# A 5x5 convolution written as 64x64 tensor tiles, with one PSUM bank's halves exchanged

## Chip, cores and metric

The kernel runs on one core of one Trainium2 chip. The metric is the device time of one launch in microseconds (us). All data are float32.

## What is computed

Four layers, each of the form x = x + f(normalised x), on a tensor of 8 batches, 32 channels, 256 rows, 256 columns. The change lies in layer 1, fused with the end of layer 0:

```python
x = x + _L0_conv_ref(_gn(x), ...)            # Fourier layer, 32x32 kept modes
x = x + _L1_conv_ref(_gn(x), kernel, 1, 2)   # layer 1: the same 5x5 kernel for every channel
x = x + _L2_conv_ref(_gn(x), ...)            # recurrence along the columns
x = x + _L3_conv_ref(_gn(x), ...)            # running maxima in four directions, mixed

def _gn(v, G=16, eps=1e-5):                  # groups of two channels
    m, s = mean(g), var(g)                   # over the group's channels and the image
    return (g - m) / sqrt(s + eps)

out = lax.conv_general_dilated(Xf, kernel[None, None], window_strides=(1, 1), padding=[(2, 2), (2, 2)])
```

## The kernel before

The program has four stages: `forward_and_mix` (forward transform and spectral product), `inverse_and_conv` (inverse transform of layer 0 and the whole of layer 1), `recurrence` (layer 2) and `maxima_and_mix` (layer 3). Only `inverse_and_conv` changes. All four keep the order written in the program: within an engine nothing overtakes anything, and the framework adds the semaphore waits.

**Data.** An image is cut into nine blocks of 32 columns that overlap by four, so that 28 of each are new. A partition is (row modulo 4, column in the block): four groups of 32 partitions. The 64 other rows, `q`, lie along the free dimension, with a zero at either end. Eight channels of nine blocks form one buffer `x1`; five such buffers rotate. A unit `u` is 16 channels of a batch, that is two buffers (`ch` 0 and 1); there are 16 units. A group of two channels is one step `g`, 0 to 7, and a step works on 9 blocks x 2 channels x 64 rows = 1152 columns.

**Convolution.** Because a partition holds row modulo 4 and column, the 5x5 kernel is a 128x128 matrix on one column of data, plus a correction for the taps that reach into the row group before or behind. In step `g`, `conv_within` (line 469) multiplies with the whole 128x128 matrix into three PSUM banks of 256, 512 and 384 columns (`BANKS`), and `conv_across` (line 477) adds the correction by two 64x64 matrices per bank, from the lower 64 partitions into the upper and the other way, with the data shifted by one row. Then VectorE (line 488) computes x = PSUM * r + x in place, with r the reciprocal standard deviation and a running sum of the result, and ScalarE (`squares2`, line 494) sums the squares. The PSUM tiles `vp` have four buffers, handed out in turn, three to a step.

**The inverse transform of the next unit** goes on beside it. `over_rows` (line 408, on `tp`, one buffer, copied out by ScalarE) works on the unit two ahead. `transform(u + 1, p, ...)` calls `over_columns` for block `p` (line 425, eight 64x32 matmuls into the two buffers of `up`), and VectorE adds the old x (line 433). `BEFORE` and `BEHIND` place the nine transforms of a unit: those of `BEFORE[g]` stand between `conv_within` and `conv_across`, those of `BEHIND[g]` after `conv_across`. `scale` (lines 456 to 462) computes r; `statistics` (lines 519 to 536) the moments for layer 2, with a power on GpSimd in it; `spectrum` (lines 366 to 380) prepares a batch's spectrum, in every second unit. SyncE's queue stores the finished buffers (line 507), GpSimd's queue loads the old x (line 387).

Of the kernel before, what the change touches and what calls it, by code (L numbers as in the profile page):

```python
# [9 lines left out]
F32 = mybir.dt.float32  # L10
AF = mybir.ActivationFunctionType
ALU = mybir.AluOpType
# [4 lines left out]
P = 128  # L17
# [7 lines left out]
Q = H // A  # L25
# [275 lines left out]
def inverse_and_conv(tc, k, d, smd, xmean, x2d, stb, first):  # L301
# [12 lines left out]
    BANKS = ((0, 2), (2, 6), (6, 9))  # L314
    PIECES = ((0, 3), (3, 6), (6, 9))

    BEFORE = ((0,), (2,), (4,), (6,), (7,), (8,), (), ())
    BEHIND = ((1,), (3,), (5,), (), (), (), (), ())
    with ExitStack() as ctx:
        one = ctx.enter_context(tc.tile_pool(name="a2c", bufs=1))  # L320
        xp = ctx.enter_context(tc.tile_pool(name="a2x", bufs=1))
# [18 lines left out]
        def x1_of(u, ch):  # L340
            return x1s[(2 * u + ch) % 5][0]

        def pair_of(u, ch, g, lo, hi, q0=1, rows=slice(0, P)):

            return x1s[(2 * u + ch) % 5][1][rows, 2 * lo : 2 * hi, g, q0 : q0 + Q]
# [71 lines left out]
        def over_columns(u, p, tag="up", bufs=2):  # L417


            tt = state[u]["tt"]  # L420
            ups = [ps.tile([P, CH * Q], F32, name=f"up_{u}_{p}_{ch}", tag=tag, bufs=bufs) for ch in range(2)]
            for a in range(A):
                for ch in range(2):
                    r = slice(64 * ch, 64 * ch + 64)
                    nc.tensor.matmul(  # L425
                        ups[ch][32 * a : 32 * a + 32],
                        lhsT=k.gw[r, p, :],
                        rhs=tt[r, a].rearrange("p c q -> p (c q)"),
                        start=True,
                        stop=True,  # L430
                    )
            for ch in range(2):
                nc.vector.tensor_tensor(  # L433
                    x1_of(u, ch)[:, p, :, 1 : 1 + Q],
                    ups[ch].rearrange("p (c q) -> p c q", q=Q),
                    xs.pop((u, ch, p)),
                    ALU.add,
                )

        def squares(u, ch, n, lo, hi, vector=False):  # L440
# [21 lines left out]
            nc.gpsimd.tensor_tensor(r, ve, k.mhalf[:, :G], ALU.pow)  # L462
            state[u]["r"][ch] = r

        def conv_within(u, ch, g):
            vps = []
            for lo, hi in BANKS:
                vp = ps.tile([P, 2 * (hi - lo), Q], F32, name=f"vp_{u}_{ch}_{g}_{lo}", tag="vp", bufs=4)
                nc.tensor.matmul(vp, lhsT=k.conv[:, 0:P], rhs=pair_of(u, ch, g, lo, hi), start=True, stop=False)  # L469
                vps.append(vp)  # L470
            return vps

        def conv_across(u, ch, g, vps):
            for (lo, hi), vp in zip(BANKS, vps):

                for r, o, q0 in ((slice(0, 64), slice(64, 128), 2), (slice(64, 128), slice(0, 64), 0)):
                    nc.tensor.matmul(  # L477
                        vp[o],
                        lhsT=k.conv[r, P : P + 64],
                        rhs=pair_of(u, ch, g, lo, hi, q0, r),  # L480
                        start=False,
                        stop=True,
                    )
            s1 = state[u]["s1"]
            srcs = ((0, 1, vps[0][:, 0:2]), (1, 2, vps[0][:, 2:4]), (2, 6, vps[1]), (6, 9, vps[2]))
            for n, (lo, hi, src) in enumerate(srcs):
                x = pair_of(u, ch, g, lo, hi)
                nc.vector.scalar_tensor_tensor(  # L488
                    x, src, state[u]["r"][ch][:, g : g + 1], x, ALU.mult, ALU.add, accum_out=s1[:, 0, n, ch, g : g + 1]
                )  # L490

        def squares2(u, ch, g):
# [19 lines left out]
        def statistics(u):  # L512
# [17 lines left out]
            nc.vector.tensor_tensor(ve, st[:, 1], ve, ALU.subtract)  # L530
            nc.vector.tensor_scalar(ve, ve, 0.0, EPS, ALU.max, ALU.add)
            nc.gpsimd.tensor_tensor(st[:, 1], ve, k.mhalf[:, :n8], ALU.pow)
            for kind in range(2):
                nc.vector.tensor_copy(
                    by_pair(stb[:, kind, b, 2 * CH * h : 2 * CH * (h + 1)]), twice(st[:, kind], 2)
                )
# [15 lines left out]
        with tc.manual_schedule(engines=None):  # L552
# [18 lines left out]
                scale(0, ch, 3)  # L571
            for u in range(n):
                for g in range(2 * G):
                    vps = conv_within(u, g // G, g % G)
                    if u + 1 < n:
                        for p in BEFORE[g]:
                            transform(u + 1, p, u + 2)
                    conv_across(u, g // G, g % G, vps)
                    if u + 1 < n:
                        for p in BEHIND[g]:  # L580
                            transform(u + 1, p, u + 2)
                    squares2(u, g // G, g % G)
                    if g == 1 and u > 0:
                        scale(u, 1)
                    if g == 2:
                        if u > 0:
                            statistics(u - 1)
                        if u % 2 == 0 and u + 2 < n:
                            spectrum(units[u + 2][0])
                    if g == G and u + 2 < n:  # L590
                        begin(u + 2)
                    if g >= G and u + 2 < n:
                        over_rows(u + 2, 2 * (g - G))
                    if g == 5 and u + 1 < n:
                        squares(u + 1, 0, 1, 1, NT)
                    if g == 7 and u % 2 and u + 3 < n:
# [5 lines left out]
                if u + 1 < n:  # L602
                    scale(u + 1, 0)
                    squares(u + 1, 1, 1, 1, NT)
            statistics(n - 1)
            store(n - 1, 1)


def recurrence_weights(tc, pool, d):
# [525 lines left out]
```

## Time and profile before

| | |
|---|---|
| Time of three runs, median (lowest to highest) | 3248.49 us (3248.48 to 3251.19) |
| Profiled execution, its own time | 3246.24 us |
| Profiled execution, span | 3244.4 us |
| Mean granted TensorE clock | 0.937 |
| Stage of the change: first conv matmul to the last evacuation | 359.4 to 1149.6 us |
| TensorE busy in 359.4 to 1112.9 us | 750.0 of 753.5 us |
| VectorE busy there | 417.0 us |
| ScalarE busy there | 427.5 us |
| DMA engines' share there | 0.72 |

Engine names in the lines: PE is TensorE's matmuls, PEld its weight loads, DVE VectorE, ACT ScalarE, POOL GpSimd, SP SyncE. A busy PE means that some matmul was under way by a modelled end, not that the array was full. A float32 matmul appears as two records. "64*64" in a line is the part of the array used; "x12" the number of records merged into the line. The profiled span is 4.1 us below the median of the runs.

### The profile page before, as it was taken

To read this page: it belongs to the slowest core of one execution; us is meant where nothing else is said; L and a number is where in the kernel's file an instruction comes from. 1 tells how busy PE (TensorE), PEld (TensorE's weight loads), DVE (VectorE), ACT (ScalarE), POOL (GpSimd) and SP (SyncE) were. 2 spreads that over 40 slices of the span, in tenths; PEclk is the share of its full clock that TensorE was granted. 3 is DMA by queue.
4 is the path that set the end of the run, shared out by engine and by line. 5 is a ranking of instruction groups with operands and counts; after the bars stand their busy time and mean duration, and the time that the engine had idled before them with its cause. 6 is when DMAs were issued, how large, how long until landed. Compare 5 with 4: busy or idle time off the path is not lost.

```text
span 3244.4 us, 107343 instructions
## 1 busy us (share of the span) xinstructions
PE 2925.4 (90%) x45498; PEld 1658.2 (51%) x45498; DVE 2503.5 (77%) x4932; ACT 1851.6 (57%) x4362; POOL 861.9 (27%) x1241
## 2 busy tenths in 40 slices
PE   7975899999999969999999999999999577777776
PEld 4664344444443446666666666666666233333332
DVE  5742555555555548999999999899989799999998
ACT  3422456465564657888888888888888222222222
POOL 0110111111111135555555555555555200000000
PEclk9985899999999989999999999999999798888888
DMA  9978577687777546655555566665554577888885
GB/s 388 384 291 188 152 187 177 186 195 193 189 174 187 118 121 159 153 143 148 147 146 146 148 154 158 158 158 152 141 147 122 181 308 310 313 312 311 308 307 219
DMA packets 527038, 655.44 MB, mean 202 GB/s; under 512 B 388825, under 2 KB 389737, under 8 KB 500829
## 3 DMA queue, kind: packets, MB, share of 16 engines
q1 hardware_dynamic: 483628, 494.33, 53.9%
q0 software_dynamic: 17200, 85.05, 7.9%
q10 hardware_dynamic: 25728, 69.21, 5.4%
q8 instruction: 356, 5.83, 0.7%
q14 instruction: 126, 1.02, 0.1%
HBM read 371.63 MB, written 272.63 MB: 199 GB/s over the span
## 4 chain that ended last, share of the span: by engine, by line
PE 69%; DVE 20%; issue 4%; DMA 3%; SPq 1%; ACT 1%; POOL 0%; DVEq 0%; ACTq 0%; POOLq 0%
PE r L696 13%; PE z L696 12%; PE vp L469 8%; PE vp L477 8%; PE ni L696 6%; PE nh L696 6%; DVE rv L947 5%; PE up L425 4%; PE yp L131 3%; DVE dq L959 2%; DVE m L963 2%; DVE m L961 2%; DVE x L956 2%; DVE m L962 2%; PE tp L408 2%
## 5 line engine op out<-in xcount | busy, mean ns | idle before, releaser
L704 PE MATMUL z<-hs,weights 64*64 64x256 f32 x4080 | 540.8, 382 | 0.0
L704 PE MATMUL r<-hs,weights 64*64 64x256 f32 x4080 | 529.4, 375 | 1.6 <-issue 1.4
L704 PE MATMUL ni<-hs,weights 64*64 64x256 f32 x4080 | 528.0, 375 | 0.0
L786 POOL TENSOR_TENSOR xw<-xw,hs 128x256 f32<-128x256 f32 x496 | 339.4, 684 | 638.4 <-DVE hs L785 636.7
L993 ACT ACTIVATE ot<-o,bres 128x512 f32<-128x512 f32 x256 | 154.9, 688 | 541.6 <-PE o L977 536.4
L494 ACT ACTIVATE junk<-x 128x128 f32<-128x128 f32 (+1 forms) x384 | 202.7, 528 | 329.8 <-DVE x L488 323.4
L977 PE MATMUL o<-m,wsc 32*32 32x512 f32 x3072 | 242.8, 855 | 154.8 <-DVE m L963 109.0
L780 POOL TENSOR_TENSOR a<-zm,xn 128x256 f32<-128x256 f32 x510 | 372.3, 730 | 7.9 <-issue 6.2
L778 ACT ACTIVATE n<-n,bih 128x256 f32<-128x256 f32 x510 | 259.2, 508 | 188.9 <-DVE n L777 188.9
L433 DVE TENSOR_TENSOR x<-up,xb 128x512 f32<-128x512 f32 x288 | 185.2, 686 | 211.9 <-PE up L425 208.3
L696 PE MATMUL z<-xn,weights 64*64 64x256 f32 x2040 | 305.4, 376 | 23.8 <-ACT xn L676 23.8
L696 PE MATMUL r<-hs,weights 64*64 64x256 f32 x2040 | 319.0, 389 | 5.4 <-DVE hs L785 4.5
L488 DVE SCALAR_TENSOR_TENSOR x<-vp,r,x 128x128 f32<-128x128 f32 (+2 forms) x512 | 236.9, 514 | 110.3 <-PE vp L477 110.1
L696 PE MATMUL r<-xn,weights 64*64 64x256 f32 x2040 | 305.3, 376 | 1.4 <-ACT rs L771 1.4
L696 PE MATMUL z<-hs,weights 64*64 64x256 f32 x2040 | 305.9, 376 | 0.0
L696 PE MATMUL nh<-xn,weights 64*64 64x256 f32 x2040 | 305.7, 376 | 0.0
L696 PE MATMUL ni<-hs,weights 64*64 64x256 f32 x2040 | 305.0, 375 | 0.0
L469 PE MATMUL vp<-x,c_conv 128*128 128x256 f32 (+2 forms) x768 | 290.3, 512 | 1.9 <-DVE x L488 1.8
L704 PEld LDWEIGHTS ni<-hs,weights 64*64 64x64 f32 x4080 | 289.5, 133 | 3.0
L676 ACT ACTIVATE xn<-xw,shift,turned 128x256 f32<-128x256 f32 x496 | 290.6, 586 | 0.0
L704 PEld LDWEIGHTS r<-hs,weights 64*64 64x64 f32 x4080 | 282.5, 131 | 6.6 <-issue 4.9
L772 DVE SCALAR_TENSOR_TENSOR n<-nh,bhh,rs 128x256 f32<-128x256 f32 x510 | 246.4, 483 | 48.6 <-ACT rs L771 34.7
(167 smaller groups left out, 6585.9 us busy)
## 6 DMA issues: line engine op xcount, KB each, us to landing
xb<-in_xl_dram POOLq DMA_DIRECT2D x96, 768.0 KB, 5.9
xa<-in_xt_dram SPq DMA_DIRECT2D x64, 1024.0 KB
x<-x3d SPq DMA_DIRECT2D x32, 2048.0 KB
fw<-fwd SPq DMA_DIRECT2D x32, 2048.0 KB
out_dram<-ot ACTq DMA_DIRECT2D x64, 1024.0 KB
xw<-x2d SPq DMA_DIRECT2D x31, 2048.0 KB
fwd<-fm SPq DMA_DIRECT2D x248, 256.0 KB
x3d<-xw SPq DMA_DIRECT2D x248, 256.0 KB
```

The source lines that it names most:

```text
L469: nc.tensor.matmul(vp, lhsT=k.conv[:, 0:P], rhs=pair_of(u, ch, g, lo, hi), start=True, stop=False)
L477: nc.tensor.matmul(vp[o], lhsT=k.conv[r, P : P + 64], rhs=pair_of(u, ch, g, lo, hi, q0, r), start=False, stop=True,)
L488: nc.vector.scalar_tensor_tensor(x, src, state[u]["r"][ch][:, g : g + 1], x, ALU.mult, ALU.add, accum_out=s1[:, 0, n, ch, g : g + 1])
L494: nc.scalar.activation(junk[:, : 2 * (hi - lo)], pair_of(u, ch, g, lo, hi), AF.Square, accum_out=state[u]["s1"][:, 1, n, ch, g : g + 1],)
L676: nc.scalar.activation(norms[bi][:, b, w], raws[bi][:, b, w], AF.Identity, bias=shift[:, b : b + 1], scale=sc[:, 1, b : b + 1])
L696: ins = nc.tensor.matmul(out[r], lhsT=weights[r, kind, gate, :], rhs=src[r], start=start, stop=stop)
L704: ins = nc.tensor.matmul(out[pairs[1 - i]], lhsT=weights[r, kind, gate, :], rhs=prev[r, :, q0 : q0 + Q], start=False, stop=stop,)
L772: nc.vector.scalar_tensor_tensor(m, p["nh"], bhh[:, 2:3], r, ALU.add, ALU.mult)
L778: nc.scalar.activation(m, m, AF.Tanh, bias=bih[:, 2:3])
L780: product = nc.gpsimd.tensor_tensor(a, zm, cur, ALU.mult)
L786: nc.gpsimd.tensor_tensor(raw, raw, new, ALU.add)
L977: nc.tensor.matmul(pts[b2][i][32 * j : 32 * j + 32].rearrange("p (w q) -> p w q", q=Q), lhsT=wsc[q, b2, t, :], rhs=src[j][q, b2], start=first,
```

## The change

The 128x128 matrix is no longer used whole. For each of the three banks there are three kinds of 64x64 pair: kind 0, the two diagonal quarters of the matrix; kind 1, its two off-diagonal quarters; kind 2, the old corrections. Each pair takes two of the four 64x64 tiles of the array: either the two diagonal ones (rows of the lower half to outputs in the lower half, upper to upper) or the two crosswise ones. In the middle bank (512 columns) the two halves of the output are exchanged, so that its kinds 1 and 2 use the diagonal tiles and its kind 0 the crosswise ones. In program order diagonal and crosswise pairs of different banks alternate. A semaphore orders the pairs that add into one bank from different rows.

The evacuation has five VectorE instructions instead of four, in the order bank 2, middle bank (two of 64 partitions, each reading PSUM from the other half than the one it writes), bank 0 (two). The transforms come after a step's convolution, and where a step has two of them (steps 1, 2 and 3), `scale`, `statistics` or `over_rows` stands between. `over_rows` for the unit two ahead starts at step 3 instead of 4. `statistics` is split: its last two copies (`keep`) come after `squares2`.

```diff
-    BEFORE = ((0,), (2,), (4,), (6,), (7,), (8,), (), ())
-    BEHIND = ((1,), (3,), (5,), (), (), (), (), ())
+    PLACES = ((0,), (1, 2), (3, 4), (5, 6), (7,), (8,), (), ())
...
-        def conv_within(u, ch, g):
...
-        def conv_across(u, ch, g, vps):
...
+        pairs = (slice(0, 64), slice(64, 128))
+        sem, count = tc.alloc_semaphore("conv_tiles"), [0]
+        some = [False]
+        def free(ins):
+            if some[0]:
+                tc.declare_no_dep(ins.ins, group="conv", reason="later matmuls of the same bank end last")
+        def conv(u, ch, g):
+            vps = [
+                ps.tile([P, 2 * (hi - lo), Q], F32, name=f"vp_{u}_{ch}_{g}_{lo}", tag="vp", bufs=4) for lo, hi in BANKS
+            ]
+            def tiles(bank, kind, start=False, stop=False, signal=False, wait=None):
+                lo, hi = BANKS[bank]
+                for i, r in enumerate(pairs):
+                    o = pairs[i if kind == 0 else 1 - i]
+                    to = pairs[i if (kind == 0) != (bank == 1) else 1 - i]
+                    ins = nc.tensor.matmul(
+                        vps[bank][to],
+                        lhsT=k.conv[r, P : P + 64] if kind == 2 else k.conv[r, o],
+                        rhs=pair_of(u, ch, g, lo, hi, (2, 0)[i] if kind == 2 else 1, r),
+                        start=start,
+                        stop=stop,
                     )
+                    if wait is not None and i == 0:
+                        ins._wait_ge(sem, wait)
+                if signal:
+                    ins.then_inc(sem, 1)
+                    count[0] += 1
...
+            tiles(1, 1, start=True)
+            tiles(2, 1, start=True)
+            second = tiles(2, 2, signal=True)
+            first = tiles(1, 2, signal=True)
+            tiles(0, 1, start=True)
+            tiles(2, 0, stop=True, wait=second)
+            third = tiles(0, 2, signal=True)
+            tiles(1, 0, stop=True, wait=first)
+            tiles(0, 0, stop=True, wait=third)
             s1 = state[u]["s1"]
-            srcs = ((0, 1, vps[0][:, 0:2]), (1, 2, vps[0][:, 2:4]), (2, 6, vps[1]), (6, 9, vps[2]))
...
+            for n, lo, hi, src, o, rows in (
+                (3, 6, 9, vps[2], everywhere, everywhere),
+                (2, 2, 6, vps[1], pairs[1], pairs[0]),
+                (2, 2, 6, vps[1], pairs[0], pairs[1]),
+                (0, 0, 1, vps[0][:, 0:2], everywhere, everywhere),
+                (1, 1, 2, vps[0][:, 2:4], everywhere, everywhere),
+            ):
+                x = pair_of(u, ch, g, lo, hi, rows=rows)
+                free(
+                    nc.vector.scalar_tensor_tensor(
+                        x, src[o], r1[rows, g : g + 1], x, ALU.mult, ALU.add, accum_out=s1[rows, 0, n, ch, g : g + 1]
+                    )
                 )
...
-                    vps = conv_within(u, g // G, g % G)
-                    if u + 1 < n:
-                        for p in BEFORE[g]:
-                            transform(u + 1, p, u + 2)
-                    conv_across(u, g // G, g % G, vps)
-                    if u + 1 < n:
-                        for p in BEHIND[g]:
-                            transform(u + 1, p, u + 2)
-                    squares2(u, g // G, g % G)
+                    conv(u, g // G, g % G)
+                    places = PLACES[g] if u + 1 < n else ()
+                    for p in places[:1]:
+                        transform(u + 1, p, u + 2)
                     if g == 1 and u > 0:
                         scale(u, 1)
+                    if g == 2 and u > 0:
+                        st = statistics(u - 1)
+                    if g == G - 1 and u + 2 < n:
+                        begin(u + 2)
+                    if G - 1 <= g < 2 * G - 1 and u + 2 < n:
+                        over_rows(u + 2, 2 * (g - G + 1))
+                    for p in places[1:]:
+                        transform(u + 1, p, u + 2)
+                    squares2(u, g // G, g % G)
                     if g == 2:
                         if u > 0:
-                            statistics(u - 1)
+                            keep(u - 1, st)
...
-                    if g == G and u + 2 < n:
-                        begin(u + 2)
-                    if g >= G and u + 2 < n:
-                        over_rows(u + 2, 2 * (g - G))
...
-            statistics(n - 1)
+            keep(n - 1, statistics(n - 1))
             store(n - 1, 1)
+            tc.declare_fence(nc.tensor.drain().ins, group="conv")
```

## The prediction

> **What bounds the kernel now.** I read the slices first, then the costly groups, then the stage's timeline by engine. In the page, "PE" is TensorE's busy share in fortieths of the span and "PEclk" its granted clock.
>
> ```profile
> PE   7975899999999969999999999999999577777776
> PEclk9985899999999989999999999999999798888888
> ...
> L433 DVE TENSOR_TENSOR x<-up,xb 128x512 f32<-128x512 f32 x288 | 185.2, 686 | 211.9 <-PE up L425 208.3
> ...
> L488 DVE SCALAR_TENSOR_TENSOR x<-vp,r,x 128x128 f32<-128x128 f32 (+2 forms) x512 | 236.9, 514 | 110.3 <-PE vp L477 110.1
> ```
>
> The stage (slices 5 to 14) has PE at 9 throughout, and VectorE's idle time in it is ended by PE: the stage is bound by TensorE. One step (g = 6, start us, us):
>
> ```profile
> 705.14 1.08 PE L408 MATMUL tp<-c_eh,spec 128*64 128x256 f32 x8
> 706.15 2.22 PE L469 MATMUL vp<-x,c_conv 128*128 128x256 f32 x6
> 708.30 2.17 PE L477 MATMUL vp<-x,c_conv 64*64 64x256 f32 x12
> 710.41 1.08 PE L408 MATMUL tp<-c_eh,spec 128*64 128x256 f32 x8
> ```
>
> By start times: whole matrix 2.15 us, corrections 2.11, an `over_rows` 1.01, a transform 1.02. From step to step I read 6.27, 6.76, 7.85, 5.25, 6.28, 6.29, 5.26 and 5.74 us in an undisturbed odd unit: 49.7 us. An even one has `spectrum` as well (step 2: 8.51), 50.4. The last unit, without transforms, has 4.25 a step.
>
> Now the hand-over between VectorE and TensorE at a step's end:
>
> ```profile
> 688.02 0.33 DVE L488 SCALAR_TENSOR_TENSOR x<-vp,r,x 128x128 f32<-128x128 f32 x1
> 688.29 0.07 DVE L488 DVE_READ_ACCUMULATOR x<-vp,r,x 128x1 f32 x1
> ...
> 688.56 0.07 DVE L488 DVE_READ_ACCUMULATOR x<-vp,r,x 128x1 f32 x1
> 688.56 0.73 DVE L488 SCALAR_TENSOR_TENSOR x<-vp,r,x 128x512 f32<-128x512 f32 x1
> ...
> 688.78 1.76 PE L469 MATMUL vp<-x,c_conv 128*128 128x512 f32 x4 [0.17 <-DVE x L488]
> ...
> 689.23 0.60 DVE L488 SCALAR_TENSOR_TENSOR x<-vp,r,x 128x384 f32<-128x384 f32 x1
> ```
>
> From start to start an evacuation of 128, 512 and 384 columns takes 0.27, 0.67 and 0.54. At 688.78 the next step's middle bank starts 0.15 after the accumulator read (688.56 + 0.07) of bank 0: with three tiles a step on four `vp` buffers, **a step's middle bank gets the buffer of the step before's bank 0**, its bank 2 that of the middle bank. Today bank 0 is evacuated first, so this costs 0.17 us.
>
> Four tiles at once are seen in the recurrence:
>
> ```profile
> 1800.51 0.38 PE L696 MATMUL ni<-hs,weights 64*64 64x256 f32 x2
> 1800.52 0.38 PE L704 MATMUL z<-hs,weights 64*64 64x256 f32 x2
> 1800.72 0.38 PE L696 MATMUL ni<-hs,weights 64*64 64x256 f32 x2
> 1800.74 0.38 PE L704 MATMUL z<-hs,weights 64*64 64x256 f32 x2
> ```
>
> Both pairs advance every 0.215 us, different data on the same rows included: 256 columns cost two such passes, 0.43 us, for all four tiles.
>
> **What the Trainium skill says.** "TensorEngine Tiling (Array Packing)", Key Properties: tiles work independently, a change of tiling mode drains the engine. Agreed: 0.43 us for four; at a change I find about 0.09 us without streaming and a first pass longer by 0.05. "TensorE: Matmul & The Clock Gate", What's actually happening: half clock after an idle window of 3.4 us, windows running free. The trace has it (PE busy, ..., granted clock):
>
> ```profile
> 578.63:582.04 3.41, 3.14 (x28) 2.66 (x21) 2.21 (x9) 1.05 (x2) 1.74 (x3) 1.00 0.72 133
> 582.04:585.45 3.41, 3.41 (x20) 0.63 (x18) 1.89 (x8) 0.00 (x0) 1.04 (x1) 0.50 0.96 367
> ```
>
> The first window holds the 8-column `statistics` matmuls, busy but hardly streaming. Counting columns only (0.83 ns a column and pass), the trace's windows fall to half at a streaming share up to 0.34, never from 0.45 on, and return at 0.83. So about **2.07 us without streaming within one window** decide (1.88 to 2.25). Three such dips occur in the stage before; one cost step 3 of a unit 6.87 instead of 5.25, 1.6 us. "VectorE: DVE Perf Modes", Two Vector instructions with no wait between them: an instruction whose operands start in another quadrant waits until those before have finished. Line 284's copies over four quadrants agree: 0.417 long, 0.430 apart, where line 433's are 0.672 long and 0.60 apart.
>
> **The change, part by part.**
>
> *TensorE's convolution.* Removed: 2.15 + 2.11 = 4.26 us a step. Added: nine pairs. By 1.68 ns a column (0.43 / 256), the crosswise tiles have 384 + 384 + 256 + 256 + 512 = 1792 columns, 3.01 us; the diagonal ones 1664, and their last pair waits for `third` (2.15 + 0.25 of drain and semaphore, as between the signal at 1800.31 and its waiter at 1800.77 in the recurrence), so ends by 2.96. The waits for `second` and `first` are satisfied before their tiles come free. With the first pass's 0.05: **3.06 us, 1.2 less**. Semaphores cost 0 (behind streaming) to 0.1; I take 0. If unequal pairs overlap worse, more (a rival).
>
> *Evacuation.* Removed 1.75 us, added 2.42: half of the partitions costs as much as all, since line 284's 32-partition copies of 256 elements take 0.42. Reading crosswise is in no row: from 0.67 (the 128x512 row) to double; I take 0.67. Two changes of quadrant wait for the accumulator: 0 to 0.16 (accumulator to line 433's start at 718.15), I take 0.10 each. Bank 2 ends early enough. The middle bank's last pass starts at 2.58 + 0.05, ends 0.59 later by the modelled end, VectorE starts 0.06 after: 3.28. Then 0.67 + 0.10 + 0.67 + 0.10 + 2 x 0.27 + 0.08: **5.44**. Bank 0 is now evacuated *last*, and the next step's first matmul wants its buffer: it starts at 5.44 + 0.15 = **5.59**, whatever TensorE has meanwhile (1.0 to 2.1 us of transform and `over_rows`, done by 5.3). Behind that waiting matmul TensorE's whole queue stands.
>
> *Two transforms in a step.* The first one's additions (line 433) stand behind the five evacuations: they start 0.16 after the last accumulator read, at 5.52, and end at 6.20 and 6.81. The second transform needs both `up` buffers: 6.96, plus 0.91, plus the mode change 0.09: the next step at **7.96**. `scale` (0.5), `statistics` (1.6) and `over_rows` (1.0) between hide in that wait: they cost nothing, and save nothing.
>
> *Sum of a unit.* Steps 0, 4, 5, 6, 7 at 5.59 and 1, 2, 3 at 7.96: 51.8, against 49.7: **+2.1**. Even units add `spectrum`: 0.24 of TensorE, and 1.9 of VectorE that delays step 3's evacuation by 0.8: 52.9 against 50.4. Units 0 to 13: before 707.8 by the start of unit 14; after 7 x 51.8 + 7 x 52.9 + 2 (the first step's wait for r, as today) = 735: +27. Unit 14 (45.7 before, no `over_rows`): +6. The last unit: 36.7 before to its last evacuation, now 7 x 5.59 + 5.44 = 44.6: +8, and 1 for its squares, as the bank that `squares2` reads first is now last. Together **+42**, the three old dips already taken out.
>
> *Clock.* Without streaming: 2.5 us before the next step at step 7 (3.06 to 5.59, small `scale` matmuls within) and 2.3 before the second transform's first tile at steps 1 and 2. For a stretch L the chance is (3.41 + L - 2 x 2.07) / 3.41: 0.53 and 0.46 twice, 1.45 dips a unit of 1.65 us: x 15 = 36; the last unit some 4 dips, 7. **+43**, from 0 if the threshold is missed.
>
> *Moved along.* ScalarE (427 of 753 us) and the stores keep their order; no DMA issue is added on SP's queue; on POOL's the loads follow transforms 2, 5, 8, a step later at most and a unit ahead of their use. `over_rows` at step 3 needs `spectrum`'s last write about 1 us before; the final drain is one instruction.
>
> Sum: 3246.2 (the profiled execution) + 42 + 43 = **3331 us**; the median stands 2.2 above that execution, within my rounding.
>
> **Rivals.** *Slower without dips* (0.17): +20 (no quadrant waits) to +42: 3266 to 3288. *TensorE stays the bound* (0.12 with all degrees of it): if the evacuation's tail after the last matmul were hidden, a unit would be 8 x 3.2 + 9 x 1.02 + 4 x 1.02 + 2.6 = 41.5, 8 us less, with the last unit -130: 3116. It decides in the tail of 2.5 us from 3.06 to 5.59: 0.27 less (2.1 / 8) makes an odd unit even without dips, below 1.1 it is gone. For it: PE is the bound today. Against: bank 0's buffer, seen at 688.78. *It nets out* within 0.2% (0.05). *The tiles don't run four at once* with unequal columns, or crosswise reads cost double (0.08): two at a time the pairs stream 3456 columns, 5.8 us, +2.7 a step, +350: about 3590; doubled reads +172. Against: the recurrence's 0.215. *The likeliest, stalls with dips* (0.58): 3290 to 3385.
>
> **The numbers.** 3331, range 3240 to 3390: it reaches down through the case without dips and past equality; outside lie most of the faster case and of the lost overlap. A measurement of this kernel tells about 0.2% (6.5 us) from no change. Faster 0.12, same 0.05, slower 0.83.
>
> **What would show it.** Right: PE in the stage falls from 0.99 to about 0.75 busy; line 433's wait for PE shrinks; the convolution's matmuls wait for DVE at the evacuation, some 2 us in most steps; steps of about 5.6 and 8.0 us; evacuations of 64x512 at about 0.75; half-clock windows in slices 5 to 14. Wrong: steps under 5.3 us; no wait of the middle bank's first matmul for bank 0; a convolution over 3.4 us; PEclk at 9 throughout with the time unchanged.

## The result, and the profile after

The changed kernel takes **3228.07 us** (median of four runs, 3227.97 to 3230.66) beside 3248.84 us for the kernel before: ratio 0.9936, 95% interval 0.9919 to 0.9954, 0.6% faster. The prediction, 3331 us with 3240 as its lower end, was wrong in sign: it had the kernel slower. The profiled execution took 3228.1 us, its span 3226.3.

The page of the changed kernel, its slices and two costly groups (TensorE's tenths, its granted clock; then busy us, mean ns, idle us before and what ended it):

```profile
PE   7975799999999969999999999999999577777776
PEclk9985899999999989999999999999999788888998
...
L527 DVE SCALAR_TENSOR_TENSOR x<-vp,r,x 64x512 f32<-64x512 f32 (+2 forms) x640 | 350.8, 563 | 164.6 <-PE vp L490 137.8
...
L490 PE MATMUL vp<-x,c_conv 64*64 64x384 f32 (+2 forms) x4608 | 457.5, 514 | 0.2
```

TensorE is still at 9 in the whole slices of the stage, since a tenth hides the difference: from 360 to 1135 us it is busy for 731 of 775 us, where it was for 772. VectorE's busy time there rose from 426 to 546 us. The convolution's matmuls have 0.2 us of idle time ahead of them in the whole run: the wait of some 2 us in most steps that the prediction looked for is not there. What TensorE's weight loads (PEld) and matmuls (PE) did wait for in the stage, from the waits of the changed kernel (us in total, times, longest):

```profile
PEld up L424 <- DVE x L433: 73.8, 93, 2.7
...
PE up L424 <- DVE x L433: 38.5, 36, 1.8
...
PEld vp L490 <- DVE x L527: 5.4, 7, 0.9
...
DVE x L433 <- DMA x2d<-x: 2.9, 1, 2.9
```

The transforms (`up`, line 424) wait for the additions (line 433); the convolution (`vp`, line 490) hardly waits for its evacuation (line 527).

From convolution start to convolution start, in us:

| Step | 0 | 1 | 2 | 3 | 4 | 5 | 6 | 7 | unit |
|---|---|---|---|---|---|---|---|---|---|
| before, odd unit | 6.27 | 6.76 | 7.85 | 5.25 | 6.28 | 6.29 | 5.26 | 5.74 | 49.7 |
| predicted | 5.59 | 7.96 | 7.96 | 7.96 | 5.59 | 5.59 | 5.59 | 5.59 | 51.8 |
| after, undisturbed odd unit (7) | 4.34 | 7.83 | 7.83 | 7.82 | 5.35 | 5.35 | 4.34 | 3.85 | 46.7 |
| after, mean of odd units 1 to 13 | 4.34 | 8.83 | 8.87 | 8.04 | 5.36 | 5.35 | 4.34 | 3.85 | 49.0 |

The stage, from the first convolution to the last evacuation, fell from 790.3 to 774.3 us, 16.0 of the 20.8 us gained. The recurrence, whose code is the same, took 4.8 us less; over all the profiled executions below it takes 1378.6 to 1386.0 us with no relation to the edit, so I read nothing into it, and compare stages and steps where a few us matter.

**The hand-over at a step's end.** The timeline of the changed kernel, VectorE and then TensorE (start us, us, engine, line, operation):

```profile
655.57 0.62 DVE L527 SCALAR_TENSOR_TENSOR x<-vp,r,x 128x384 f32<-128x384 f32 x1 [1.48 <-PE vp L490]
656.11 0.09 DVE L527 DVE_READ_ACCUMULATOR x<-vp,r,x 128x1 f32 x1
656.22 0.75 DVE L527 SCALAR_TENSOR_TENSOR x<-vp,r,x 64x512 f32<-64x512 f32 x1
656.91 0.08 DVE L527 DVE_READ_ACCUMULATOR x<-vp,r,x 64x1 f32 x1
657.00 0.75 DVE L527 SCALAR_TENSOR_TENSOR x<-vp,r,x 64x512 f32<-64x512 f32 x1
...
657.79 0.35 DVE L527 SCALAR_TENSOR_TENSOR x<-vp,r,x 128x128 f32<-128x128 f32 x1
```

```profile
652.85 3.38 PE L490 MATMUL vp<-x,c_conv 64*64 64x512 f32 x36
656.16 0.61 PE L457 MATMUL v<-sq,c_valid 128*128 128x4 f32 x4
656.70 3.27 PE L490 MATMUL vp<-x,c_conv 64*64 64x512 f32 x34
```

At 656.70 the next step's first matmul, the middle bank's, starts without a wait. By then VectorE has evacuated bank 2 alone; the evacuation of bank 0, whose buffer that matmul was predicted to wait for, begins at 657.79.

**A step with two transforms**, TensorE of the changed kernel:

```profile
661.04 3.38 PE L490 MATMUL vp<-x,c_conv 64*64 64x512 f32 x36
664.35 1.09 PE L424 MATMUL up<-tt,c_gw 64*32 64x512 f32 x16
665.37 0.61 PE L457 MATMUL v<-sq,c_valid 128*128 128x4 f32 x4
667.25 2.27 PE L424 MATMUL up<-tt,c_gw 64*32 64x512 f32 x16 [1.27 <-DVE x L433]
669.45 3.32 PE L490 MATMUL vp<-x,c_conv 64*64 64x512 f32 x24
```

VectorE in the same step, and the second transform of the same step in the undisturbed unit 7:

```profile
666.51 1.28 DVE L433 TENSOR_TENSOR x<-up,xb 128x512 f32<-128x512 f32 x2
```

```profile
716.33 1.68 PE L424 MATMUL up<-tt,c_gw 64*32 64x512 f32 x16 [1.27 <-DVE x L433]
```

The second transform starts at 667.25, after the first of VectorE's two additions, which stand behind all five evacuations (they run from 666.51). That is the predicted stall. In unit 7 the second transform takes 1.68 us and not 1.09, because its second buffer waits for the second addition; here it takes 2.27. Two adjoining windows of the changed kernel (busy us of PE, PEld, DVE, ACT, POOL; granted clock; DMA share; GB/s) show the reason for the other 0.6 us.

```profile
664.80:668.21 3.41, 2.14 (x29) 0.83 (x20) 3.01 (x11) 3.16 (x17) 0.20 (x1) 1.00 0.81 107
668.21:671.62 3.41, 3.41 (x29) 1.38 (x18) 1.29 (x2) 3.22 (x13) 1.67 (x3) 0.50 1.10 137
```

The window with the stall is followed by one at half clock. There are 20 such stretches in the stage, 72 us in all; the kernel before had 3, 10 us.

### The profile page after: what moved, and what is told of

It is laid out like the page before. It is cut to its first block, busy times and chain, and to the rows that moved or that the text cites. A ratio compares the mean times of both kernels' runs of the same rounds, so it can differ in the third digit from the quotient of the medians.

```text
span 3226.3 us, 112014 instructions
## 1 busy us (share of the span) xinstructions
PE 2866.3 (89%) x47802; PEld 1666.4 (52%) x47802; DVE 2614.3 (81%) x5188; ACT 1862.5 (58%) x4362; POOL 860.8 (27%) x1241
## 4 chain that ended last, share of the span: by engine, by line
PE 54%; DVE 25%; DMA 8%; SPq 6%; issue 5%; ACT 2%; POOL 0%; DVEq 0%; ACTq 0%; POOLq 0%
PE r L742 13%; PE z L742 12%; PE ni L742 6%; PE nh L742 6%; DMA x2d<-x 6%; SPq L547 5%; DVE rv L993 5%; PE vp L490 4%; DVE x L527 3%; PE yp L131 3%; DVE dq L1005 2%; DVE m L1009 2%; DVE m L1007 2%; DVE x L1002 2%; DVE m L1008 2%
## 5 line engine op out<-in xcount | busy, mean ns | idle before, releaser
L527 DVE SCALAR_TENSOR_TENSOR x<-vp,r,x 64x512 f32<-64x512 f32 (+2 forms) x640 | 350.8, 563 | 164.6 <-PE vp L490 137.8
L490 PE MATMUL vp<-x,c_conv 64*64 64x384 f32 (+2 forms) x4608 | 457.5, 514 | 0.2
L490 PEld LDWEIGHTS vp<-x,c_conv 64*64 64x64 f32 x4608 | 238.3, 138 | 234.5 <-issue 128.5
L817 ACT ACTIVATE rs<-r,brz 128x256 f32<-128x256 f32 x510 | 242.7, 476 | 50.8 <-PE r L750 30.3
```

Of the source, the lines that this page charges most:

```text
L490: ins = nc.tensor.matmul(vps[bank][to], lhsT=k.conv[r, P : P + 64] if kind == 2 else k.conv[r, o], rhs=pair_of(u, ch, g, lo, hi, (2, 0)[i] ...
L527: nc.vector.scalar_tensor_tensor(x, src[o], r1[rows, g : g + 1], x, ALU.mult, ALU.add, accum_out=s1[rows, 0, n, ch, g : g + 1])
L817: rs = nc.scalar.activation(r, p["r"], AF.Sigmoid, bias=brz[:, 0:1])
```

## The experiments

Each ratio is to the kernel before, run beside it. "Unit" means the table's last column; the floor of a step is its length where it loses nothing to half clock or to a late store. SyncE's stores, `x1` to `x2d`, are 72 in a unit.

### Which buffer does a bank get? Three buffers for `vp`

```diff
-tag="vp", bufs=4
+tag="vp", bufs=3
```

> Three accumulator buffers instead of four. The theory on record (each bank inherits a fixed bank's buffer of the step before, in a rotation): with three, the middle bank inherits the middle bank's own buffer, which VectorE lets go 4.82 us after its convolution began, so no step is shorter than 4.97 us: steps 0 and 6 rise by 0.6, step 7 by 1.1, about +2.4 us per unit, 3228 + 36 = 3264 us, and the first matmul of a step (middle bank) is the one that waits. Rival (the bank used first by TensorE gets the buffer released the earliest): the middle bank gets bank 2's old buffer, free at 3.4 us, and does not wait; bank 2's first matmul, 0.43 later in its step, gets the middle bank's, free at 4.82: steps not below 4.54, +0.2 in steps 0 and 6, +0.7 in step 7, about +1.1 us per unit, 3228 + 17 = 3245 us. Steps 1 to 3 do not change under either.

Measured: 3250.12 us, ratio 1.0000 (0.9992 to 1.0008), between the two theories, so that the time alone doesn't decide. Step 6 stays at 4.34, step 7 rises to 4.37, step 0 to 5.36, and step 1 from 7.83 to 8.46, which neither theory had. Step 0 of unit 7, TensorE and then VectorE of this kernel:

```profile
713.39 4.41 PE L490 MATMUL vp<-x,c_conv 64*64 64x512 f32 x36
717.73 1.09 PE L424 MATMUL up<-tt,c_gw 64*32 64x512 f32 x16
```

```profile
712.78 0.08 DVE L527 DVE_READ_ACCUMULATOR x<-vp,r,x 128x1 f32 x1
...
714.42 0.08 DVE L527 DVE_READ_ACCUMULATOR x<-vp,r,x 64x1 f32 x1
...
715.08 0.08 DVE L527 DVE_READ_ACCUMULATOR x<-vp,r,x 128x1 f32 x1
```

The first matmul starts at 713.39, after bank 2's evacuation (712.78) and before those of the middle bank (714.42) and of bank 0 (715.08) are over. Two of the three buffers still hold what VectorE has yet to read, so it has bank 2's. The convolution is stretched inside, from 3.39 to 4.41 us: its second bank starts at 714.55, 0.05 us after the middle bank's last accumulator read ends. So the rival holds: the bank that TensorE uses first gets the buffer that was let go the earliest. I had its size off: step 0 lost 1.0 us, not 0.2, and step 1 0.6, not 0.

### The two halves of the change: places, and exchange

The old convolution, with its own evacuation in four instructions, in the new places:

```diff
-                    conv(u, g // G, g % G)
+                    conv_across(u, g // G, g % G, conv_within(u, g // G, g % G))
```

> The convolution of the kernel before (4.26 us, with its two halves one behind the other) with the new places of transforms, scale, statistics and over_rows. Theory (the places cost, the convolution gains): steps with one transform or none as before, 6.28, 6.28, 5.26, 5.7 us; steps 1 to 3 wait for `up` behind the last evacuation at about 5.3 and the additions to 6.6: 7.65 us or more each where the kernel before has 6.76, 7.85 and 5.25; about +3 us per unit, 3249 + 40 = 3290 us, and 60 us slower than the changed kernel. Rival (the new places bring the gain, since no transform delays a convolution's second half): 3249 us or less.

Measured: 3264.12 us, ratio 1.0047 (1.0035 to 1.0060). Steps 1 to 3 of an odd unit are 7.80, 7.95 and 7.80 us instead of 6.76, 7.85 and 5.25: the places cost, as expected. Steps 0 and 7 are 1.0 us shorter, each having handed a transform or an `over_rows` to another step; I had left that out, so the loss is 15 us and not 40. Of the change, then, the places cost 15 us, and the tiled convolution with its evacuation brings 36 in those places (by the stage alone, 808.2 us in this kernel, 18 and 34).

Without the exchange of the middle bank:

```diff
-                    to = pairs[i if (kind == 0) != (bank == 1) else 1 - i]
+                    to = pairs[i if kind == 0 else 1 - i]
...
-                (2, 2, 6, vps[1], pairs[1], pairs[0]),
-                (2, 2, 6, vps[1], pairs[0], pairs[1]),
+                (2, 2, 6, vps[1], everywhere, everywhere),
```

> The changed kernel without the exchange of the middle bank's halves: in all three banks kinds 1 and 2 run in the crosswise tiles and kind 0 in the diagonal ones, and VectorE evacuates in four instructions. Working of the prediction: the crosswise tiles then stream 2 x 1152 columns instead of 1792, 3.87 us by 1.68 ns instead of 3.01, so a convolution takes 3.9 to 4.15 us; steps 0 and 4 to 7 rise by 0.6 to 0.8, while the chain of evacuations is one instruction (0.7 us) shorter and ends about where it did, so steps 1 to 3 stay: +3 to +4 us per unit, 3228 + 50 = about 3278 us if nothing else takes it up, 3250 if the waits for stores do. Rival (the crosswise reading costs as much as it brings): 3228 us within 5.

Measured: 3328.78 us, ratio 1.0248 (1.0234 to 1.0262), 101 us over the changed kernel and twice the expected 50. From the timeline of this kernel:

```profile
686.38 1.09 PE L424 MATMUL up<-tt,c_gw 64*32 64x512 f32 x16
687.40 1.08 PE L407 MATMUL tp<-c_eh,spec 128*64 128x256 f32 x8
688.42 4.85 PE L490 MATMUL vp<-x,c_conv 64*64 64x512 f32 x36
```

A convolution takes 4.8 us, more than the columns of the crosswise tiles (3.87). The diagonal pairs must each wait for their bank's crosswise pairs and have no work before that: by the single records the last crosswise pass starts at 692.16, its 256 columns are through by 692.38, and bank 0's diagonal pair runs alone from 692.67 to about 693.1, 0.7 of the missing 0.9 us. The crosswise reading costs VectorE 0.7 us a step and gives TensorE 1.5.

### The convolution's own length

```diff
-            tiles(2, 0, stop=True, wait=second)
             third = tiles(0, 2, signal=True)
+            tiles(2, 0, stop=True, wait=second)
```

> The changed kernel, with the crosswise pair (0, 2) of bank 0 ahead of the diagonal pair (2, 0) of bank 2 instead of behind it. Theory: a convolution takes 3.32 us and not the 3.06 worked out, because the last pair (0, 0) stands behind (1, 0)'s second pass, which waits for its tiles, and the weights of (0, 0) are issued only then; in the new order the last pair's semaphore is older and its tiles free: convolution 3.1 us, steps 0 and 4 to 7 shorter by 0.2 each, but bank 2's evacuation starts 0.2 us later, so steps 1 to 3 grow by 0.2: -0.4 us per unit, about 3222 us. Rival (the columns themselves take longer when four tiles run at once): 3.32 us stays, and 3228 to 3238 us.

Measured: 3227.04 us, ratio 0.9936 (0.9922 to 0.9949), in time no gain on the changed kernel. By their modelled ends bank 0's last pair is through 3.13 us after the convolution's start instead of 3.38, but the middle bank's last pass, at 3.28, now comes last; from start to start the single steps fall by 0.12, not 0.2. So the order of the last pairs did hold the end up, by 0.12 of the 0.25 over 3.06. Most of the rest is the change of tiling behind the convolution: in step 6 of unit 7 of this kernel the last pass's columns are through 3.11 us after the start (512 columns at 0.83 ns from 751.435, an estimate), and the next matmul, of another tiling, starts at 3.20. Steps 1 to 3 keep a floor of 7.8 to 7.95.

### Taking the wait for `up` away, and what took its place

VectorE's order, with the evacuations cut off from `conv` into a function of their own:

```diff
+                    cut = 3 if len(places) > 1 else 5
+                    evacuate(u, g // G, g % G, vps, slice(0, cut))
                     for p in places[:1]:
                         transform(u + 1, p, u + 2)
+                    evacuate(u, g // G, g % G, vps, slice(cut, 5))
```

> In the three steps with two transforms VectorE's order is changed: the first transform's two additions stand ahead of bank 0's two evacuations. If the second transform waits for the two `up` buffers behind all five evacuations (theory), their release comes about 0.55 us earlier (two instructions of some 0.25 us fewer ahead of it), steps 1 to 3 fall from 7.82 at the floor to about 7.3, 3 x 14.3 x 0.55 = 23 us: about 3205 us, a little less if half-clock stretches go with it. Rival (the next step's first matmul waits for bank 0's buffer, evacuated last): bank 0 comes later now, steps 1 to 3 stay or grow by up to 1.3 us: 3228 to 3280 us.

Measured: 3224.63 us, ratio 0.9915 (0.9898 to 0.9931). The floor of steps 1 to 3 did fall, to 7.28, as the theory had it. But the mean of step 1 in odd units rose from 8.83 to 10.91: a new wait.

One more matmul between the two transforms:

```diff
+                    if len(places) > 1:
+                        warm = ps.tile([P, CH * Q], F32, name=f"warm_{u}_{g}", tag="st")
+                        nc.tensor.matmul(warm, lhsT=k.conv[:, 0:P], rhs=..., start=True, stop=True)
```

> One more matmul, 128x128 on 512 columns into the statistics bank, its result unread, stands between the two transforms of steps 1 to 3, in the time in which TensorE waits for `up`. If the half-clock stretches in the stage (22 of them in the profile of the changed kernel) come from these waits, most of them go, steps 1 to 3 go from means of 8.7, 8.9 and 8.3 us to near their floor of 7.82, and the time falls by up to 36 us: 3195 to 3210 us. Rival (the stretches have another cause, or the time is set by VectorE's chain whatever the clock): no change, 3228 us, or up to 10 us more where the extra matmul ends after the wait.

Measured: 3226.68 us, ratio 0.9929 (0.9907 to 0.9951). Of the half-clock stretches 3 are left, and the even units fall from 49.8 to 48.1. Yet step 1 of the odd units rose to 11.28 on average.

The first of two transforms inside the convolution:

```diff
             tiles(0, 1, start=True)
+            for p in between:
+                transform(u + 1, p, u + 2)
             tiles(2, 0, stop=True, wait=second)
```

> New convolution, but in the steps with two transforms the first one stands inside the convolution (ahead of the tiles that wait, as in the kernel before) and the second behind it, so that its additions run on VectorE before the evacuations, while VectorE has nothing to do. If the wait for `up` behind the evacuations is what costs (theory), it is gone: steps 1 and 2 are TensorE's 5.36 us or VectorE's 5.9 to 6.2 (five evacuations of some 3.2 us and four additions of 0.67), step 3 about 6.4, 18 us together where 23.5 are the floor now and 26.0 the mean; with the half-clock stretches gone as well 3228 - 14.3 x 8 = about 3115 us, without that 3150. Rival (next step's first matmul waits for bank 0's evacuation, 2.3 us behind the convolution's end): steps 1 to 3 about 6.9 to 7.4 each, 3155 to 3200 us.

Measured: 3220.32 us, ratio 0.9901 (0.9885 to 0.9918). The steps are as the theory had them where they run free: 6.8, 7.65 and 6.53 us. And again step 1 of the odd units is long, 14.5 us on average, up to 18.1. VectorE's timeline in such a step, and a line of the waits, both of this kernel:

```profile
709.87 0.69 DVE L433 TENSOR_TENSOR x<-up,xb 128x512 f32<-128x512 f32 x1 [7.67 <-DMA x2d<-x]
```

```profile
DVE x L433 <- DMA x2d<-x: 43.7, 8, 8.6
```

An addition writes into an `x1` buffer whose last holder's store has not landed. The same wait is 2.9 us in the changed kernel, 23.1 with VectorE's order changed and 16.8 with the extra matmul. SyncE's timeline of this kernel:

```profile
689.72 69.31 SPq L549 DMA_DIRECT2D x2d<-x  x112
```

112 stores in 69.3 us without a break, 0.62 us each: at that rate 72 are 44.6 us, and every second unit has four loads of the spectrum in the same row. In all three kernels a unit takes 49.4 to 49.9 us on average, whatever its steps' floors.

### Is it SyncE's row, or the DMA engines?

The kernel with a transform inside the convolution, without the loads of x (units 2 to 15 use unit 1's tiles again):

```diff
             for ch in range(2):
+                if u > 1:
+                    for p in range(lo, hi):
+                        xs[u, ch, p] = kept[ch, p]
+                    continue
```

> The kernel with the first of two transforms inside the convolution, without the loads of x in units 2 to 15 (the additions take unit 1's tiles again, so part of the data is another). The loads are 768 KB each, six in a unit. Theory (the stores' rate is what bounds: SyncE can issue one in 0.46 us, but while a load runs the 16 DMA engines are full and the row stands): without loads 72 stores take some 33 us, no addition waits for a store, units fall to 44.2 and 45.2 us, the stage to about 700 us and the time to some 3150 us. Rival (SyncE's own pace, with its waits for the store eight earlier, is the bound): step 1 of the odd units keeps its wait, 3205 us or more.

Measured: 3156.26 us, ratio 0.9720 (0.9707 to 0.9734), as the theory had it: units of 44.3 and 45.0, no wait for a store. From 500 to 1050 us SyncE waits 58.3 us for earlier stores to land in the kernel with the loads, and not once in the one without. So it is the loads that make the stores late. That they do it by filling the DMA engines fits the DMA share of the kernel with loads, 1.02 in 690 to 695 us, where a load runs, and 0.58 in 705 to 710, but no run here separates it from other ways in which a load can slow a store. The rate was not quite as expected: without loads a store takes 0.52 us in SyncE's unbroken rows of more than 20, with them 0.56, so 72 take 37 us and not 33.

16 stores of a unit from ScalarE, in three kernels: the changed one, the one with a transform inside the convolution, the one before. `store` puts those of two blocks on a list, and `store_late(n)` issues the next n of it by `nc.scalar.dma_start`:

```diff
+                    if p in (2, 6) and u < n - 1:
+                        late.append((b, a, c0, t, lo, hi, u, ch, p))
+                        continue
...
                     squares2(u, g // G, g % G)
+                    store_late(2)
```

> The changed kernel with 16 of a unit's 72 stores to x2d (blocks 2 and 6) issued by ScalarE, two behind each step's squares, instead of by SyncE. Theory: SyncE's row of stores (one in some 0.46 us when the queue takes them, about 490 of 500 us occupied in the trace of the changed kernel) is the next bound, some 48 to 50 us per unit, and stands just behind the stage of the changed kernel: here only the one long step (11.6 us, an addition that waits for a store) goes, 3 to 10 us less: about 3221 us. The wait for `up` and the half-clock stretches stay. Rival (the stores are no bound; ScalarE's issues, 0.9 us per step, delay its copies and squares): 3228 to 3240 us.

> The kernel with the first of two transforms inside the convolution, with 16 of a unit's 72 stores issued by ScalarE as well. There the wait for `up` had gone from steps 1 to 3 (6.8, 7.4 and 6.5 us), but step 1 of the odd units waited up to 12 us for a store. Theory (SyncE's row of stores had become the bound): with it relieved the odd units fall to 44.2 us and the even ones to about 45.2, 14 x 4.5 us less than the changed kernel's 49.3: 3228 - 63 = about 3160 us. Rival (the 16 DMA engines are what is full, whoever issues): the waits stay, about 3215 to 3225 us.

> The kernel before, with the same 16 stores of a unit issued by ScalarE. If TensorE bounds the stage of the kernel before (prediction), nothing comes of it: 3249 us within 5, or a few us more where ScalarE's copies are late. Rival (SyncE's row of stores, some 48 to 50 us per unit, bounds the kernel before too, and TensorE only fills the same time): the time falls, by up to 20 us.

Measured, in this order: 3333.98 (ratio 1.0262, 1.0248 to 1.0276), 3285.78 (1.0110, 1.0097 to 1.0124) and 3380.00 us (1.0398, 1.0384 to 1.0412). All three are slower than either theory had it. SyncE's waits, first in the changed kernel and then in the same with ScalarE's stores:

```profile
SPq L547 <- DMA x2d<-x: 80.9, 70, 3.1
```

```profile
SPq L551 <- DMA x2d<-x: 335.0, 95, 14.3
```

SyncE now stands for up to 14 us for a store to land ahead of issuing its next. In the records of these runs ScalarE's stores signal the same eight semaphores as SyncE's (110 to 117 in the first), so that one row waits for the other's turn; GpSimd's signal eight others (101 to 108 in the next run). These three kernels tell nothing of where the bound lies.

The same 16 stores (of units 1 to 14) from GpSimd, in the kernel with a transform inside the convolution:

```diff
-                nc.scalar.dma_start(
+                nc.gpsimd.dma_start(
...
-                    store_late(2)
+                    if g in (2, 3, 4, 5, 6):
+                        store_late(4)
```

> The same kernel with all its loads, with 16 of a unit's 72 stores (blocks 2 and 6 of units 1 to 14) issued by GpSimd, four behind each of the squares of steps 2 to 6. Moving them to ScalarE had made things worse, with SyncE idle for stretches of up to 14 us: theory, SyncE's and ScalarE's stores share the semaphores and wait for one another's; GpSimd's have their own. If so, and if SyncE's row is the bound: 3160 to 3190 us. Rival (the DMA engines are full, or GpSimd's stores stand in its row behind loads that wait for VectorE): no gain, 3220 us, or slower by up to 60 us.

Measured: **3171.91 us**, ratio 0.9775 (0.9759 to 0.9790), as the theory had it. Units of 45.8 and 45.1 us. The late stores had covered the gain, and moving some of them uncovers it.

### How the changed kernel divides

The same edit for GpSimd's stores in the changed kernel, and in the one with the extra matmul:

> The changed kernel with 16 of a unit's 72 stores issued by GpSimd. Theory (in the changed kernel the wait for `up` and the half-clock stretches set the pace, and the row of stores stands just behind them): only the one long step goes, 3 us, so 3222 to 3228 us. Rival (the row of stores sets the pace of the changed kernel already): 20 us or more less.

> The same with the extra 512-column matmul between the two transforms of steps 1 to 3. It had removed nearly all half-clock stretches before (even units 50.0 to 48.06 us) while the odd units lost the gain in waits for stores. Theory (the clock costs the changed kernel some 30 us, hidden only by the stores): units of 47.1 and 48.1 us, 14 x (49.3 - 47.6) = 24 us less than the changed kernel and 20 less than k1: about 3203 us. Rival (the extra matmul costs what the clock gives): as k1.

Measured: 3221.25 (ratio 0.9908, 0.9893 to 0.9922) and 3207.06 us (0.9863, 0.9849 to 0.9878). The stores cost the changed kernel 7 us by the times, 12 by the stage (774.3 to 762.1 us), nearer to the theory than to the rival. Between these two kernels lie another 14: the half-clock stretches in the stage fall from 14 (48 us) to 2, and the extra matmul stretches step 2 from 7.83 to 8.20 us, some 5 us over all units. So the 12 stretches that went had cost about 19 us, an estimate that puts the whole difference down to these two.

### Was the kernel before bound by its stores?

The same edit in the kernel before:

> The kernel before with the same 16 stores of a unit issued by GpSimd. Theory (TensorE bounds its stage, no addition of it waits for a store): 3249 us within 5. Rival (its pace is that of the row of stores): 15 us or more less.

Measured: 3276.73 us, ratio 1.0083 (1.0069 to 1.0098), neither theory. This trial was spoilt by its own place (waits of that kernel, VectorE's copy behind `statistics`):

```profile
DVE stb L546 <- POOL st L544: 51.4, 14, 5.2
```

GpSimd's power stands behind four stores there, and VectorE behind the power; in the kernel before the same wait is 28.8 us. With the stores kept away from that step:

```diff
-                    if g in (2, 3, 4, 5, 6):
+                    if g in (3, 4, 5, 6):
```

> The kernel before with 16 of a unit's 72 stores issued by GpSimd, four behind each of the squares of steps 3 to 6, none in the step of the statistics. Theory (TensorE bounds the stage of the kernel before): the odd units keep their 49.7 us, the time is 3249 us within 8. Rival (the row of stores bounds it): 15 us or more less.

Measured: 3246.34 us, ratio 0.9997 (0.9989 to 1.0005). The kernel before was not bound by its stores. SyncE's waits from 500 to 1100 us, in the kernel before and then in the changed one, show how much nearer the change brought them:

```profile
SPq L507 <- DVE x L488: 69.5, 34, 10.8
SPq L507 <- DMA x2d<-x: 41.5, 33, 2.5
```

```profile
SPq L547 <- DMA x2d<-x: 65.3, 58, 3.1
SPq L547 <- DVE x L433: 6.1, 12, 1.4
```

Over all its waits SyncE stood 79 of 600 us for data of VectorE or TensorE before, and 14 after: its row of stores had become nearly full.

### What gained, together

A transform inside the convolution, the pair (0, 2) ahead of (2, 0), and GpSimd's stores: 24 in the first kernel (`p in (2, 4, 6)`, five behind each of the squares of steps 2 to 6), 16 in the second (four behind those of steps 3 to 6).

> All that gained together: first transform inside the convolution, pair (0, 2) ahead of (2, 0), and 24 of a unit's 72 stores (blocks 2, 4 and 6) on GpSimd. Expected by the theory: units of 44.3 and 45.0 us as without loads, less 0.12 in each of the five single steps, and the waits for stores that 16 had left (some 13 us in all) gone: 3172 - 13 - 8 = about 3150 us. Rival (GpSimd's row, 24 stores of 0.64 us, six loads and the powers, becomes late): 3172 us or more.

> The joined kernel with 16 stores of a unit on GpSimd, four behind each of the squares of steps 3 to 6. Theory (GpSimd's row of 24 stores was late in k3: step 1 took 6.7 to 9.8 us): step 1 near 6.8 us in most units, about 3155 us. Rival (16 are too few to relieve SyncE's row, as one step of 12.6 us in that kernel showed): 3163 to 3172 us.

Measured: **3163.46 us**, ratio 0.9730 (0.9715 to 0.9745), with 24 stores on GpSimd; 3169.00 us, 0.9756 (0.9743 to 0.9769), with 16. The first is the fastest full kernel of this study, 2.7% below the kernel before. Neither reached its estimate. Step 1 of the odd units still takes up to 14 us with 16, and up to 9.8 with 24, where GpSimd's stores stand 61.6 us in all behind its own loads; which of its waits makes that step long is left open. 3156 us without loads shows that little is left to gain from the stores.

## Why the prediction was wrong, step by step

- **What bounds the kernel before**: right. TensorE bounds it; the relieved stores changed nothing (0.9997).
- **"A step's middle bank gets the buffer of the step before's bank 0"**: this is the step that failed. The line at 688.78 was read rightly, but it allowed two rules. In the kernel before, the banks were requested, used and evacuated in one order, so "bank 0's buffer" and "the buffer let go the earliest" were the same thing. The change reversed the order of evacuation, and there the two part. The trace of after (656.70) excludes the first, and the trial with three buffers (713.39) shows the second; "handed out in turn", as the section on the kernel before has it, holds for that kernel's order alone. Therefore the restart at 5.59 us does not exist: steps 0 and 4 to 7 take TensorE's own 3.85 to 5.36, 23.2 us together instead of 27.95, so 4.7 us a unit, 66 us by the start of unit 14; the last unit, predicted to 44.6, took 34.1. These 76 us are most of the 103 between 3331 and 3228.
- **The evacuation chain**: right. 0.67 to 0.69 for a crosswise 64x512 and 0.09 to 0.12 of hold at a change of quadrant (656.91 to 657.00, 656.11 to 656.22) against 0.67 and 0.10; its end at 5.56 us after the convolution's start, against 5.44. It just was not what the next step waited for.
- **The convolution**: 3.31 us (652.85 to 656.16) instead of 3.06. Two terms were left out. One is the change of tiling behind it, about 0.1. The other is the order in which TensorE takes its instructions: the last pair stood behind a pass that waited for its tiles. The Trainium skill ("TensorE: Matmul & The Clock Gate", Step-by-step: what each phase is for) says that weight loads may be pulled ahead of matmuls under way while the matmuls stay in program order; this trace shows no such pull here: the last pair's weights, which wait for a semaphore, were issued at 655.57, 40 ns after the second pass of the pair before had begun, though the matmul that signals had started at 654.88, and the 0.46 us that the prediction read in the recurrence from signal to waiter would have let them go at 655.34. Exchanging two pairs gave 0.12 us of the 0.25 back per step.
- **Two transforms in a step**: right. 7.96 predicted, 7.82 measured, and 7.80 to 7.95 with the old convolution. The second transform starts after the first addition, 6.21 us into the step in unit 7, but its second buffer waits for the second one until 6.81, where 6.96 was predicted.
- **Clock**: right in mechanism, wrong in place and size. It was priced at 43 us, a part of it in step 7 and in the last unit, where there is no wait. Steps 1 to 3 alone have it: about 19 us for 12 stretches by the pair of runs with relieved stores, so some 30 for the 20 of the changed kernel, an estimate. The threshold of 2.07 us without streaming was too long: by the prediction's way of counting (columns times 0.83 ns a pass) windows of the changed kernel fell at streaming shares of 0.29 to 0.47, that is from 1.8 us without streaming on, where the trace before had none above 0.34.
- **"No DMA issue is added on SP's queue"**: true, and not enough. The row of stores was not priced as the next bound. It cost the changed kernel 7 to 12 us, but it swallowed nearly all that three further edits gained: 3220 to 3227 us where 3115 to 3210 were expected.
- **The rival "TensorE stays the bound"**, with 0.12, had the sign and these five steps: no wait of the middle bank's first matmul for bank 0, steps 0, 6 and 7 under 5.3 us, 4 and 5 at 5.35. Its 3116 us is about as far off as the prediction's number, since it had no wait for `up` in steps 1 to 3.

The sum, by the runs: the places cost 15 us; the tiled convolution in them gains 36. The measured gain is 20.8. The wait for `up`, with the half clock that it brings, was worth 49 more once the stores were relieved (3221.25 to 3171.91; by the stage 762.1 to 712.2).

## What to carry to other kernels

A wait in a trace says who released, not by what rule the buffer was chosen; before an edit that reverses an order, ask which rules the old order could not tell apart. When an edit shortens a stage by a few per cent, price the row of DMA issues that runs beside it as the next bound, and relieve it together with the edit: here two good edits, a transform inside the convolution and one more matmul, looked worthless until 16 of 72 stores had moved (VectorE's new order was not tried with them moved). A queue that shares semaphores or an engine with the critical path is a poor place to move them to.

## What I had not expected of the hardware

- Four 64x64 tiles of unequal columns overlap as well as equal ones: the 1792 crosswise columns were through in 3.11 us, where 1.68 ns each make 3.01. But TensorE's instructions still come one behind another: a waiting second pass kept another tile's pair back, 3.31 against 3.19 us from a convolution to the next matmul.
- A stretch of 1.8 us without streaming inside a window of 3.41 us can cost the clock: in the stage of the changed kernel windows with a streaming share of 0.29 to 0.47 were followed by half clock, some of 0.46 and more were not, one of 0.48 at half clock kept it, and full clock came back from 0.78 on.
- A store of 56 KB takes SyncE about 0.46 us when nothing holds it, and 0.62 on average in an unbroken row of 112 beside the loads; GpSimd issues one in 0.64 us (143.0 us for 224).
